# Layer norm statistics by accumulating passes of ScalarE beside a causal attention, and a projection that leaves PSUM by ScalarE

## The chip, the cores and the metric

The kernel runs on 1 core of one Trainium2 chip. The metric is the device time of one launch in microseconds (us). Before the change it is 2574.32 us, the median of 3 runs (2571.3 to 2575.26).

## The reference

The input x has 4096 rows of 256 numbers, all in float32. Two residual layers follow each other, and each normalises on the way in and on the way out:

```python
x = x + layernorm(attention(layernorm(x)))
x = x + layernorm(ffn(layernorm(x)))
# attention: 16 heads of 16 features, causal, softmax(q k^T / 4) v, with bias b_attn,
#            then the projection  out @ w_proj + b_proj
# ffn: silu(x w1) * (x w2), two hidden layers 1024 x 1024 with gelu, then w3 (ternary weights, scales)
# layernorm(x) = (x - mean) / sqrt(variance + 1e-5), over the 256 features
```

The change concerns two of the four layer norms: the one before the attention and the one after the projection.

## The kernel before, in words

The rows are cut into 8 query blocks of 512 rows (QB), each of 4 tiles of 128 rows (NT). The attention goes over items (j, g): query block j from 0 to 7, and within it the head groups g from 0 to 3, with 4 heads each. An item has 4(j+1) steps kt, one for each tile of 128 keys. Each step issues, in this order, on the in-order queues of the engines:

- a first unit of maxima of an item to come (`MaxUnit`, L496): two products q k on TensorE (PE) into banks pm (L508), and two row maxima by VectorE (DVE, L521; on the diagonal L525 with the mask). Per step there are two such units, so four maxima. The banks come from `ps_m`, a ring of 3.
- two score units (`ScoreUnit`, L568): products s on PE (L591), less the maximum by a second product, and the exponential on ScalarE (ACT, L606). They use the ring `ps_s` of 2 double banks. On the diagonal GpSimd (POOL) zeroes what lies beyond it (L611).
- the second unit of maxima, and then the product with v of the step before (`Values.step`, L632, matmuls av L641). When an item is done, ACT copies av to SBUF (L650) and SP sends it to DRAM (`weighed`).
- some pieces of background work, and every fourth step one piece of `halve_weights` (L665) on POOL, which rounds weights for the feed-forward.

The order is written out by hand (manual schedule); nothing is reordered afterwards. `Background` (L27) holds a list of generators with a size each. `pace` (L57) draws, at the end of each step, as many pieces as the sum of the sizes divided by the steps that are left, rounded up; these steps are those of the items up to g = 2 of the block. So the sizes in

```python
PREP, PROJECT, NORM = 22, 20, 12
```

(L183) set how many pieces a step draws, and with that when each piece is issued. Two generators run beside each query block:

- `project(j, room)` (L185) projects the block that has just been finished. It reads the sums of the softmax back from DRAM (L191), takes their reciprocal on DVE (L194), sends that to DRAM and reads it back spread out (L201), multiplies on POOL (L208), multiplies by w_proj in two halves of two tiles on PE (L218), adds the bias and takes the statistics on DVE (L226, L138, L139), and normalises and adds x on POOL (L149, L238). The PSUM bank of a half comes from `ps_s`, shared with the scores.
- `prep(j)` (L433) prepares the block two further on: layer norm statistics on DVE (L138, L139), normalising on POOL, transposes, and the products that give k, q and v (`features`, L361), whose evacuation is done by ACT (L375, L478).

Where a generator yields `BESIDE`, one unit of maxima that is due later is issued between (`unit_beside`, L741): beside query blocks 1 to 6, up to four pairs a block. The first two `prep` run before the attention begins. The last projection runs beside the feed-forward, which comes after the attention (`feed_forward`, L848).

The statistics before the change are two DVE operations for a tile, and 1/sqrt is one DVE and one POOL operation:

```python
nc.vector.bn_stats(st, src)
nc.vector.bn_aggr(mv[:, t, :], st)
...
nc.vector.tensor_scalar_add(ve, mv[:, :, 1], EPS)
nc.gpsimd.tensor_tensor(rstd, ve, neghalf, ALU.pow)
```

Of the kernel before, what the change touches and what calls it, by code (L numbers as in the profile page):

```python
# [10 lines left out]
F32 = mybir.dt.float32  # L11
F32R = mybir.dt.float32r
AF = mybir.ActivationFunctionType
ALU = mybir.AluOpType
# [3 lines left out]
P = 128  # L18
QB = 512
NT = QB // P  # L20
NEG = -1.0e30
EPS = 1e-5
# [45 lines left out]
def sandwich_kernel(  # L68
# [19 lines left out]
    nc = tc.nc  # L88
    S, D = x.shape
# [6 lines left out]
    NB = S // QB  # L96
# [4 lines left out]
    const = ctx.enter_context(tc.tile_pool(name="const", bufs=1))  # L101
# [4 lines left out]
    stat = ctx.enter_context(tc.tile_pool(name="stat", bufs=3))  # L106

    def rows(src, j):
        return src[j * QB : (j + 1) * QB, :].rearrange("(t p) d -> p t d", p=P)

    def load_block(j, src=x):
        t = xpool.tile([P, NT, D], F32, tag="x", name=f"x{j}")
        nc.sync.dma_start(out=t, in_=rows(src, j))
        return t
# [18 lines left out]
    neghalf = const.tile([P, NT], F32, tag="neghalf", name="neghalf")  # L133
    nc.gpsimd.memset(neghalf, -0.5)

    def layernorm_stats(src, mv, t):
        st = stat.tile([P, nc.vector.BN_STATS_DIM], F32, tag="bn", name="bn")
        nc.vector.bn_stats(st, src)  # L138
        nc.vector.bn_aggr(mv[:, t, :], st)  # L139

    def layernorm_rstd(mv):
        ve = stat.tile([P, NT], F32, tag="ve", name="ve")
        nc.vector.tensor_scalar_add(ve, mv[:, :, 1], EPS)  # L143
        rstd = stat.tile([P, NT], F32, tag="rstd", name="rstd")
        nc.gpsimd.tensor_tensor(rstd, ve, neghalf, ALU.pow)  # L145
        return rstd

    def normalize(dst, src, mv, rstd, t, engine=nc.vector):
        engine.tensor_scalar(  # L149
            dst, src, mv[:, t, 0:1], rstd[:, t : t + 1], ALU.subtract, ALU.mult  # L150
        )
# [27 lines left out]
    bp = const.tile([P, D], F32, tag="bp", name="bp")  # L179

    weighed = [scratch.tile([G, P, QB], F32, tag=f"av_{j}", name=f"avd_{j}") for j in range(NB)]
    inverse = [scratch.tile([H, QB], F32, tag=f"inv_{j}", name=f"invd_{j}") for j in range(NB)]
    PREP, PROJECT, NORM = 22, 20, 12  # L183

    def project(j, room):  # L185

        xj = load_block(j)

        sums = stat.tile([P, H * QB // P], F32, tag="sums", name=f"sums_{j}")
        heads = weighed[j].rearrange("g (h e) n -> (g h) e n", e=HW)  # L190
        nc.sync.dma_start(out=sums, in_=heads[:, HD, :].rearrange("h (a n) -> h a n", a=8))  # L191
        for _ in range(3):
            yield True
        nc.vector.reciprocal(sums, sums)  # L194
        yield True
        nc.sync.dma_start(out=inverse[j].rearrange("h (a n) -> (h a) n", a=8), in_=sums)
        oT, inv = room.features(j)
        for c in range(DC):
            mine = slice(8 * c, 8 * (c + 1))
            nc.sync.dma_start(out=oT[:, c, :], in_=heads[mine, 0:HD, :])  # L200
            nc.sync.dma_start(  # L201
                out=inv[:, c, :],
                in_=inverse[j][mine, None, :].to_broadcast([8, HD, QB]),
            )
        for _ in range(4):
            yield True
        for c in range(DC):
            nc.gpsimd.tensor_tensor(oT[:, c, :], oT[:, c, :], inv[:, c, :], ALU.mult)  # L208
            yield True
        for _ in range(2):  # L210
            yield True
        y = room.tokens(j)
        mv = stat.tile([P, NT, 2], F32, tag="mv", name=f"mvy_{j}")
        for half in range(0, NT, 2):
            ps = room.bank(f"py_{j}_{half}").rearrange("p (t f) -> p t f", t=2)
            for t in range(2):
                for c in range(DC):
                    nc.tensor.matmul(  # L218
                        ps[:, t, :],
                        lhsT=oT[:, c, (half + t) * P : (half + t + 1) * P],  # L220
                        rhs=wp[:, c, :],
                        start=(c == 0),
                        stop=(c == DC - 1),
                    )
                yield Background.BESIDE
            nc.vector.tensor_tensor(  # L226
                y[:, half : half + 2, :],
                ps,
                bp[:, None, :].to_broadcast([P, 2, D]),
                ALU.add,  # L230
            )
            for t in range(2):
                layernorm_stats(y[:, half + t, :], mv, half + t)
            yield True
        rstd = layernorm_rstd(mv)
        for t in range(NT):
            normalize(y[:, t, :], y[:, t, :], mv, rstd, t, nc.gpsimd)
            nc.gpsimd.tensor_tensor(y[:, t, :], y[:, t, :], xj[:, t, :], ALU.add)  # L238
            yield True
        nc.sync.dma_start(out=rows(x1[j], 0), in_=y)  # L240
        yield True
# [36 lines left out]
    with ExitStack() as actx:  # L278
# [13 lines left out]
        def two_banks(name):  # L292
            return ps_s.tile([P, 2, QB], F32, tag="s", name=name)

        class Room:
# [5 lines left out]
            def features(self, j):  # L301
                return [wk1.tile([P, DC, QB], F32, tag=t, name=f"{t}_{j}") for t in ("o", "inv")]
# [130 lines left out]
        def prep(j, engine=nc.gpsimd):  # L433

            xj = xb[j] if j in xb else load_block(j)
            for _ in range(3):
                yield True
            mv = stat.tile([P, NT, 2], F32, tag="mv", name=f"mv_{j}")
            for t in range(NT):
                layernorm_stats(xj[:, t, :], mv, t)  # L440
                yield True
            v_j = kv.tile([P, NT, H * VW + HD], F32, tag=f"v{j}", name=f"v{j}")
            vb.append(v_j)
            nc.gpsimd.memset(v_j[:, :, H * VW :], 0.0)
            v_heads = v_j[:, :, 0 : H * VW].rearrange("p t (h e) -> p t h e", e=VW)
            nc.gpsimd.memset(v_heads[:, :, :, HD:VW], 1.0)
            rstd = layernorm_rstd(mv)
            for t in range(NT):
                normalize(xj[:, t, :], xj[:, t, :], mv, rstd, t, engine)
                yield True  # L450
            for _ in range(3):
                yield True
            xT = xTs[j] = wk1.tile([P, DC, QB], F32, tag="T", name=f"xT_{j}")
            ps = two_banks(f"pt_{j}")
            for c in range(DC):
                for t in range(NT):
                    nc.tensor.transpose(
                        ps[:, c, t * P : (t + 1) * P], xj[:, t, c * P : (c + 1) * P], ident
                    )
            nc.scalar.copy(xT, ps)  # L460
            yield True
            for s in "kq":
                for c in range(DC):
                    yield from features(j, s, c, engine)
                    yield True
            for half in range(0, NT, 2):
                ps = two_banks(f"pv_{j}_{half}")[:, 0, :].rearrange("p (t f) -> p t f", t=2)
                for t in range(2):
                    for c in range(DC):
                        nc.tensor.matmul(  # L470
                            ps[:, t, :],
                            lhsT=xT[:, c, (half + t) * P : (half + t + 1) * P],
                            rhs=wv[:, c, :],
                            start=(c == 0),
                            stop=(c == DC - 1),
                        )
                    yield Background.BESIDE
                nc.scalar.copy(  # L478
                    v_heads[:, half : half + 2, :, 0:HD],
                    ps.rearrange("p t (h d) -> p t h d", d=HD),  # L480
                )
                yield True
# [256 lines left out]
        ahead, begun_pair, item = [], [], (0, 0)  # L739
# [14 lines left out]
        ps = two_banks("pb")[:, 0, 0:D]  # L754
# [93 lines left out]
    def feed_forward(halves):  # L848
# [6 lines left out]
        with ExitStack() as fctx:  # L855
# [189 lines left out]
```

## Time and profile before

| | |
|---|---|
| median of 3 runs | 2574.32 us |
| the profiled execution | 2574.63 us, its span 2572.9 us |
| mean granted TensorE clock | 0.966 |
| matmuls of PE, busy | 2439.2 us (95%) |
| DVE, busy | 1824.1 us (71%) |
| ACT, busy | 1257.2 us (49%) |
| POOL, busy | 575.2 us (22%) |
| L521, maxima of 128x512 on DVE | 1792 times, 1112.4 us busy |
| L606, exponentials on ACT | 1175 times, 1040.6 us busy |
| L138, statistics of x in `prep`, `norm_block` | 64 times, 415 ns each |
| L138, statistics of y in `project` (7 blocks) | 28 times, 411 ns each |
| L139, their aggregation | 181 to 184 ns each |
| L226, bias of the projection on DVE | 14 times, 682 ns each |

A line of the profile gives the engine, the source line, the operation, what it writes and reads (`y<-py,bp`: y from py and bp), its shape and how often it occurs. In a timeline the first two numbers are the start and the duration in us, and the bracket at the end is the time for which the engine had been idle, with what ended that wait. PEld is the loading of weights into PE, SPq the queue from which DMAs are issued. The length of a step can be read from the starts of successive groups of eight av matmuls (L641): there are 4608 of them, eight for each of the 576 steps. The attention spans the first 1851 us; the feed-forward follows.

### The profile page before, as it was taken

The page shows a single profiled execution, that of the slowest core. Times are in us where ns is not written, and L with a number is a line of the kernel's source. Part 1 is how long each engine was busy: PE and PEld are TensorE (multiplying, and loading weights), DVE is VectorE, ACT ScalarE, POOL GpSimd, SP SyncE. Part 2 cuts the span into 40 slices and gives each one's busy share as a digit, 9 for nine tenths or more (in the row PEclk, how much of TensorE's full clock was granted, in tenths as well). Part 3 has the DMA queues.
Part 4 walks back from the last instruction along what each step waited for, and adds up shares of the span by engine and source line. Part 5 has one row for each costly group of instructions (what it writes and reads, how often), then busy time and mean ns, then how long its engine had stood idle before and what let it go on. Part 6 is the DMA issues. An engine that isn't in the chain of part 4 may idle for free. (4 is left out here: it accounts for less than half of the span.)

```text
span 2572.9 us, 40118 instructions
## 1 busy us (share of the span) xinstructions
PE 2439.2 (95%) x15237; PEld 1444.8 (56%) x15237; DVE 1824.1 (71%) x3965; ACT 1257.2 (49%) x1490; POOL 575.2 (22%) x869
## 2 busy tenths in 40 slices
PE   5899999999999999999999999999989999999998
PEld 2454445445445544554455554544468877887786
DVE  2687788879788987898899898986055445544553
ACT  1335466556566655666577666766712222222221
POOL 2325333332242234322322222000120000000000
PEclk8779899899999999999999999999999999999999
DMA  4444244232233323324212232111120000000000
GB/s 156 144 152 154 88 135 153 99 129 74 91 108 123 120 83 130 109 79 141 66 62 95 83 96 72 57 45 55 42 90 17 17 1 17 17 17 1 17 9 10
DMA packets 134777, 202.73 MB, mean 79 GB/s; under 512 B 14864, under 2 KB 59536, under 8 KB 134576
## 3 DMA queue, kind: packets, MB, share of 16 engines
q1 hardware_dynamic: 132624, 198.75, 23.3%
q8 instruction: 122, 2.00, 0.3%
q10 hardware_dynamic: 1776, 1.18, 0.2%
q0 software_dynamic: 176, 0.15, 0.1%
q14 instruction: 79, 0.65, 0.1%
HBM read 137.91 MB, written 62.13 MB: 78 GB/s over the span
## 5 line engine op out<-in xcount | busy, mean ns | idle before, releaser
L606 ACT ACTIVATE e<-s 128x1024 f32<-128x1024 f32 (+3 forms) x1175 | 1040.6, 936 | 618.5 <-PE s L591 611.5
L521 DVE TENSOR_REDUCE mx<-pm 128x1 f32<-128x512 f32 x1792 | 1112.4, 682 | 160.4 <-PE pm L508 145.8
L508 PE MATMUL pm<-k,q 64*128 64x512 f32 (+3 forms) x2304 | 636.8, 460 | 56.8 <-DVE mx L521 40.7
L508 PEld LDWEIGHTS pm<-k,q 64*128 64x128 f32 x2304 | 326.5, 190 | 567.3 <-DVE mx L521 394.7
L641 PE MATMUL av<-e,v 128*32 128x512 f32 (+3 forms) x4608 | 591.1, 584 | 2.9 <-POOL e L611 2.9
L591 PE MATMUL s<-q,k 64*128 64x512 f32 (+3 forms) x2304 | 476.3, 395 | 7.6 <-DVE y L226 3.1
L591 PE MATMUL s<-mrow,ones 64*128 64x512 f32 (+3 forms) x2304 | 461.6, 384 | 0.0
L525 DVE CUSTOM_DVE_ANT_0 pm<-pm,mask 128x384 f32<-128x384 f32 (+3 forms) x512 | 239.8, 517 | 75.3 <-PE pm L508 71.4
L974 ACT ACTIVATE fb<-z,sh 128x512 f32<-128x512 f32 x128 | 88.1, 688 | 396.6 <-PE z L940 377.8
L591 PEld LDWEIGHTS s<-q,k 64*128 64x128 f32 x2304 | 237.0, 191 | 79.0 <-issue 19.3
L591 PEld LDWEIGHTS s<-mrow,ones 64*128 64x128 f32 x2304 | 241.8, 191 | 38.6 <-DVE mrow L565 0.7
L611 POOL TENSOR_SCALAR_AFFINE_SELECT e<-e 128x256 f32<-128x256 f32 x256 | 102.2, 407 | 647.6 <-ACT e L606 645.9
L145 POOL TENSOR_TENSOR rstd<-ve,neghalf 128x4 f32<-128x4 f32 x32 | 32.9, 1027 | 847.7 <-DVE ve L143 822.1
L940 PE MATMUL z<-hb_0h,h 128*128 128x512 f32 x512 | 203.7, 398 | 0.0
L940 PE MATMUL z<-hb_0l,h 128*128 128x512 f32 x512 | 202.2, 395 | 0.0
L641 PEld LDWEIGHTS av<-e,v 128*32 128x32 f32 x4608 | 92.6, 109 | 148.8 <-issue 130.0
L910 DVE CAST hb_1h<-fb 128x512 fp32r<-128x512 f32 x64 | 27.4, 428 | 149.9 <-ACT fb L974 149.9
L910 DVE CAST hb_0h<-fb 128x512 fp32r<-128x512 f32 x64 | 27.5, 430 | 139.4 <-ACT fb L974 139.4
L940 PEld LDWEIGHTS z<-hb_0h,h 128*128 128x128 f32 x512 | 96.8, 189 | 22.9
L940 PEld LDWEIGHTS z<-hb_0l,h 128*128 128x128 f32 x512 | 96.8, 189 | 22.1
L959 ACT ACTIVATE sl<-za,s 128x512 f32<-128x512 f32 x64 | 44.1, 689 | 131.4 <-DVE fa L961 66.4
L693 POOL CAST wh<-wc 128x256 fp32r<-128x256 f32 x88 | 34.9, 397 | 261.8 <-DMA wc<-in_h_t_dram 197.1
(235 smaller groups left out, 2430.9 us busy)
## 6 DMA issues: line engine op xcount, KB each, us to landing
k<-k SPq DMA_DIRECT2D x288, 256.0 KB
q<-q SPq DMA_DIRECT2D x64, 256.0 KB
x<-in_x_dram SPq DMA_DIRECT2D x16, 512.0 KB
k<-hik SPq DMA_DIRECT2D x32, 256.0 KB
k<-lok SPq DMA_DIRECT2D x32, 256.0 KB
q<-hiq SPq DMA_DIRECT2D x32, 256.0 KB
q<-loq SPq DMA_DIRECT2D x32, 256.0 KB
avd<-av_sb SPq DMA_DIRECT2D x32, 256.0 KB
```

What stands on the lines that cost most here:

```text
L508: nc.tensor.matmul(ps[:, 0:n], lhsT=qT[j, g][pr][r, t * P : (t + 1) * P], rhs=kT[G * j + g, c, pr][r, 0:n], start=True, stop=True,)
L521: nc.vector.tensor_reduce(self.mx[:, h, c : c + 1], ps[:, 0:n], AX.X, ALU.max)
L525: nc.vector.tensor_tensor_reduce(out=ps[:, 0:n], in0=ps[:, 0:n], in1=mask[:, QB - n : QB], scale=1.0, scalar=-3.0e38, op0=ALU.add, op1=ALU ...
L591: nc.tensor.matmul(self.ps[i][:, self.q0 :], lhsT=(self.k, ones[pr])[m][r, :], rhs=(qT[j, g][pr], mT[j, g])[m][r, self.q0 :], start=(m == ...
L606: nc.scalar.activation(e[:, at : at + n, q0:], ps[:, :, q0:], AF.Exp)
L611: nc.gpsimd.affine_select(out=at, in_=at, compare_op=ALU.is_ge, fill=0.0, base=0, pattern=[[0, 2], [1, P]], channel_multiplier=-1,)
L641: nc.tensor.matmul(self.av[h * HW : (h + 1) * HW, q0:], lhsT=vb[kt // NT][:, kt % NT, o : o + HW], rhs=es[h // 2][:, h % 2, q0:], start=(k ...
L693: nc.gpsimd.tensor_copy(hi, w)
L910: nc.vector.tensor_copy(hi, full)
L940: nc.tensor.matmul(ps, lhsT=w[c], rhs=single(part[:, c, :]), start=(c == 0 and i == 0), stop=(c == kc - 1 and i == parts - 1),)
L959: nc.scalar.activation(sl, za, AF.Silu, scale=s1[:, oc : oc + 1])
L974: nc.scalar.activation(h, z, AF.Gelu, scale=sc[:, oc : oc + 1])
```

## The change

In `prep` for blocks 2 to 7 and in `project` for blocks 0 to 6, that is wherever they run beside the attention, the statistics are taken by two passes of ACT over each tile. The first gives minus the mean as the accumulated sum of -x/256. The second squares x plus that value, and accumulates the sum of squares. Between the two passes, and after each, the generator yields. The small operation ahead of 1/sqrt goes to POOL and does the division by 256; the normalising on POOL adds instead of subtracting. In `project` a half of the product leaves PSUM by a copy on ACT, and the bias is added on POOL, in place, in SBUF. The statistics of all four tiles come after both halves. The sizes of the two generators grow by the added yields. The first two `prep`, the last `project` and `norm_block` keep the operations of before.

```diff
+    def mean_of(src, mv, t):
+
+        junk = const.tile([P, D], F32, tag="junk", name="junk")
+        nc.scalar.activation(
+            junk, src, AF.Identity, scale=-1.0 / D, accum_out=mv[:, t, 0:1]
+        )
+
+    def spread_of(src, mv, t):
+
+        junk = const.tile([P, D], F32, tag="junk", name="junk")
+        nc.scalar.activation(
+            junk, src, AF.Square, bias=mv[:, t, 0:1], accum_out=mv[:, t, 1:2]
+        )
+
+    def rstd_of(mv):
+
+        ve = stat.tile([P, NT], F32, tag="ve", name="ve")
+        nc.gpsimd.tensor_scalar(ve, mv[:, :, 1], 1.0 / D, EPS, ALU.mult, ALU.add)
+        rstd = stat.tile([P, NT], F32, tag="rstd", name="rstd")
+        nc.gpsimd.tensor_tensor(rstd, ve, neghalf, ALU.pow)
+        return rstd
+
+    def shift_and_scale(dst, src, mv, rstd, t, engine):
+        engine.tensor_scalar(
+            dst, src, mv[:, t, 0:1], rstd[:, t : t + 1], ALU.add, ALU.mult
+        )
...
-    PREP, PROJECT, NORM = 22, 20, 12
+    PREP, PROJECT, NORM = 26, 28, 12
...
+        last = j == NB - 1
...
-            nc.vector.tensor_tensor(
-                y[:, half : half + 2, :],
-                ps,
-                bp[:, None, :].to_broadcast([P, 2, D]),
-                ALU.add,
+            if last:
...
+            else:
+                nc.scalar.copy(y[:, half : half + 2, :], ps)
+                nc.gpsimd.tensor_tensor(
+                    y[:, half : half + 2, :],
+                    y[:, half : half + 2, :],
+                    bp[:, None, :].to_broadcast([P, 2, D]),
+                    ALU.add,
+                )
+            yield True
+        if not last:
+            for t in range(NT):
+                mean_of(y[:, t, :], mv, t)
+                yield True
+                spread_of(y[:, t, :], mv, t)
+                yield True
+        rstd = (layernorm_rstd if last else rstd_of)(mv)
+        for t in range(NT):
+            (normalize if last else shift_and_scale)(
+                y[:, t, :], y[:, t, :], mv, rstd, t, nc.gpsimd
             )
-            for t in range(2):
-                layernorm_stats(y[:, half + t, :], mv, half + t)
-            yield True
-        rstd = layernorm_rstd(mv)
-        for t in range(NT):
-            normalize(y[:, t, :], y[:, t, :], mv, rstd, t, nc.gpsimd)
...
+            ahead = j < 2
             for t in range(NT):
-                layernorm_stats(xj[:, t, :], mv, t)
+                if ahead:
+                    layernorm_stats(xj[:, t, :], mv, t)
+                else:
+                    mean_of(xj[:, t, :], mv, t)
+                    yield True
+                    spread_of(xj[:, t, :], mv, t)
                 yield True
...
-            rstd = layernorm_rstd(mv)
+            rstd = (layernorm_rstd if ahead else rstd_of)(mv)
             for t in range(NT):
-                normalize(xj[:, t, :], xj[:, t, :], mv, rstd, t, engine)
+                (normalize if ahead else shift_and_scale)(
+                    xj[:, t, :], xj[:, t, :], mv, rstd, t, engine
+                )
                 yield True
```

More of the change, by code (lines that the diff above doesn't have):

```diff
@@ L225, in project @@
                 yield Background.BESIDE
-            nc.vector.tensor_tensor(
-                y[:, half : half + 2, :],
-                ps,
-                bp[:, None, :].to_broadcast([P, 2, D]),
-                ALU.add,
-            )
-            for t in range(2):
-                layernorm_stats(y[:, half + t, :], mv, half + t)
-            yield True
-        rstd = layernorm_rstd(mv)
-        for t in range(NT):
-            normalize(y[:, t, :], y[:, t, :], mv, rstd, t, nc.gpsimd)
+            if last:
+                nc.vector.tensor_tensor(
+                    y[:, half : half + 2, :],
+                    ps,
+                    bp[:, None, :].to_broadcast([P, 2, D]),
+                    ALU.add,
+                )
+                for t in range(half, half + 2):
+                    layernorm_stats(y[:, t, :], mv, t)
+            else:
+                nc.scalar.copy(y[:, half : half + 2, :], ps)
+                nc.gpsimd.tensor_tensor(
+                    y[:, half : half + 2, :],
+                    y[:, half : half + 2, :],
+                    bp[:, None, :].to_broadcast([P, 2, D]),
+                    ALU.add,
+                )
[10 more added lines that the diff above has]
+                y[:, t, :], y[:, t, :], mv, rstd, t, nc.gpsimd
+            )
             nc.gpsimd.tensor_tensor(y[:, t, :], y[:, t, :], xj[:, t, :], ALU.add)
@@ L446, in prep @@
             nc.gpsimd.memset(v_heads[:, :, :, HD:VW], 1.0)
-            rstd = layernorm_rstd(mv)
+            rstd = (layernorm_rstd if ahead else rstd_of)(mv)
             for t in range(NT):
-                normalize(xj[:, t, :], xj[:, t, :], mv, rstd, t, engine)
+                (normalize if ahead else shift_and_scale)(
+                    xj[:, t, :], xj[:, t, :], mv, rstd, t, engine
+                )
                 yield True
```

## The prediction

> **What bounds the kernel now.** I read the page's shares first, then the periods of the inner step over the whole attention, then the timeline of an ordinary step and of a step with a projection in it. The attention runs from about 40 to 1851 us of the span; the feed-forward after it holds no line that the change touches outside its last-block branch, so it stays as it is.
>
> ```profile
> PE 2439.2 (95%) x15237; PEld 1444.8 (56%) x15237; DVE 1824.1 (71%) x3965; ACT 1257.2 (49%) x1490; POOL 575.2 (22%) x869
> 908.00:927.00 19.00, 19.00 (x146) 9.70 (x142) 17.25 (x35) 14.01 (x15) 6.18 (x8) 1.00 0.48 145
> 927.00:948.00 21.00, 17.90 (x90) 8.49 (x92) 16.21 (x38) 6.56 (x8) 2.90 (x3) 0.92 0.00 1
> ```
>
> The second and third lines are windows: busy PE, PEld, DVE, ACT and POOL, then the granted clock. In seven ordinary steps PE is full, VectorE (DVE) has 9% left and ScalarE (ACT) 26%. In the next 21 us, with one projection, PE, DVE and ACT are all idle part of the time: they wait for each other. Ordinary step, timeline:
>
> ```profile
> 923.21 2.48 DVE L521 TENSOR_REDUCE mx<-pm 128x1 f32<-128x512 f32 x4 [0.21 <-PE pm L508]
> 923.74 1.94 ACT L606 ACTIVATE e<-s 128x1024 f32<-128x1024 f32 x2 [0.76 <-PE s L591]
> 924.38 0.16 PEld L641 LDWEIGHTS av<-e,v 128*32 128x32 f32 x8 [0.25 <-issue]
> 925.38 0.18 PEld L508 LDWEIGHTS pm<-k,q 64*128 64x128 f32 x2 [0.84 <-DVE mx L521]
> 925.91 2.48 DVE L521 TENSOR_REDUCE mx<-pm 128x1 f32<-128x512 f32 x4 [0.22 <-PE pm L508]
> ```
>
> The period is 925.91 - 923.21 = 2.70 us: four maxima at 0.62 (2.48) and 0.22 of waiting for the next products, while ACT does two exponentials (1.94) and waits 0.76. PE and DVE bound each other through the three PSUM banks of pm. The step with half a projection:
>
> ```profile
> 927.09 1.06 PE L641 MATMUL av<-e,v 128*32 128x512 f32 x8
> 931.16 1.29 DVE L521 TENSOR_REDUCE mx<-pm 128x1 f32<-128x512 f32 x2 [0.20 <-PE pm L508]
> 932.36 0.68 DVE L226 TENSOR_TENSOR y<-py,bp 128x512 f32<-128x512 f32 x1
> 932.90 2.14 ACT L606 ACTIVATE e<-s 128x1024 f32<-128x1024 f32 x2 [4.52 <-PE s L591]
> 933.08 0.43 DVE L138 BATCH_NORM_STATS2 bn<-y 128x6 f32<-128x256 f32 x1
> 934.07 0.18 DVE L139 BATCH_NORM_AGGREGATE mvy<-bn 128x2 f32<-128x6 f32 x1
> 934.17 0.54 DVE L525 CUSTOM_DVE_ANT_0 pm<-pm,mask 128x384 f32<-128x384 f32 x1
> 934.82 0.18 PEld L508 LDWEIGHTS pm<-k,q 64*128 64x128 f32 x1 [1.14 <-DVE mx L525]
> 935.20 1.06 PE L641 MATMUL av<-e,v 128*32 128x512 f32 x8
> ```
>
> From 932.36 to 934.17 DVE does the bias addition and the statistics; behind them stand the maxima, whose bank PE needs at 934.82, and behind that the next av. This is the stretch that the change empties.
>
> **What the Trainium skill says.** "ScalarE: Activation LUTs", section What ACT_TABLE_LOAD costs: 186 ns and 0.833 ns per element, some 93 more for each pointer operand. The trace agrees: 382 ns for 256 elements of e (399 by the rule), 687 for 512 with a bias pointer (706). "VectorE: DVE Perf Modes", section Two Vector instructions with no wait between them: an operation that also writes its accumulator is two instructions; here 141 ns for DVE's read. For ScalarE's no run here shows it. "TensorE: Matmul & The Clock Gate", Part 1: the clock falls to half after an idle window of about 3.4 us. The trace has such pieces of 3.4 and 6.8 us, one at 943.6, just after a projection. "SBUF — State Buffer", section Who interferes with whom: DVE disturbs GpSimd (POOL) only with two SBUF inputs or in its two-port modes; the maxima read PSUM, so I charge nothing.
>
> **The change, part by part.** The profiled execution took 2574.63 us (span 2572.9), 0.3 above the median 2574.32; I sum against it. (j,g) is query block and head group, a step one kt; blocks are named by the attention that runs (beside block j, block j-1 is projected).
>
> 1. Projection halves, 14. Per half, 0.68 (L226), twice 0.43 (L138) and twice 0.18 (L139), 1.81 in all overlapped, leave DVE. The block's maxima then follow at 932.45; the bank is free 0.62 later, PE's second pm of that unit at 933.3 and av at 933.55 instead of 935.20: 1.65 less. The next half (943.44 - 935.20 = 8.24) comes to the same 6.5: 1.75 less. The features' steps, built alike but evacuated by ACT, take 6.31 and 6.43 (av at 1001.57, 1007.88, 1014.31), which speaks for it. Blocks 1 to 6: 6 x 3.4 = 20.4. Block 7 has no maxima units slipped between (steps of 6.04 and 5.98); the second pm moves from 1551.82 to 1550.75: 2 x 1.1 = 2.2. Together -22.6. The new PSUM copy is L650's kind (593 ns for 128x512) and runs at about 930.7 to 931.3, in ACT's 4.52 of waiting: nothing; without that cover 14 x 0.59 = 8. The bank is given back earlier than by L226.
> 2. Half-clock pieces after projections: the excess of steps over their like is 2.3 in block 3, 1.5 in 5, 1.6 and 1.3 in 6: 6.7. With PE idle less, I take -5 (0 to -6.7).
> 3. Preparation of blocks 2 to 7: 24 pairs of statistics leave DVE. A step with one takes 2.92 instead of 2.70: the pair's 0.44 fills the 0.22 first. Where DVE is never idle the whole 0.44 counts: 24 x 0.22 to 0.44 = 5.3 to 10.6. With 13 of L143's 0.16, I take -8.
> 4. ACT: 52 mean and 52 spread passes over 256 elements. 0.38 to 0.47 by the rows above, the spread with its bias pointer, and an accumulator read that I price as DVE's 0.14: 0.55 and 0.65. Below: 0.38 (no separate read). Above: 1.0, if the read and the wait of the spread for the mean cost 0.3 more. From block 3 on one goes into each step, behind both exponentials: 0.65 against 0.76 of waiting. It costs nothing there; e is read by av a step later (e ended 1.4 before av), and its bank is wanted 0.5 after it is free, so even 0.85 would only pile up slowly. In blocks 1 and 2 the larger sizes (28 and 26) draw two or three pieces a step: some 16 steps with two passes, 1.25 - 0.76 = 0.5 over, 8; less the 0.5 of slack in each of four rows and the longer steps of block 1: +4 (0 to 10). The built program has no further table load.
> 5. POOL: 14 additions over 128x512, 1.28 each by L208's row, and 13 small operations (0.1 to 1.0). POOL is 22% busy and had been idle 24.8 us before it worked on this projection. Behind the addition stand the casts of the weights and the next selects; ACT's first mean waits for it, but a step (2.7 us) lies between. The scaling moves past diagonal steps in blocks 4 to 6 and leaves them in block 3: 0 (-1 to +4).
> 6. Moved pieces. The order of the built program has the reciprocal (L194) one step earlier in blocks 1 and 3, the projection three steps earlier in block 1 (kt 4 instead of 7) and five in block 3. Its transfers come no earlier: in SP's queue the sums' read stands behind the landing of av. DVE waited 0.37 and 1.22 there; now a step more, 2 x 2.7. In block 1 the products for c=1 are ready at 176.1 (L208), and PE would arrive near 172.7: 3.5 of stall. In block 3 they are ready at 460.6, PE comes at 460.7: nothing. Sum +9 (0 to 12). Such waits brought half-clock pieces in blocks 2, 4 and 6 (waits of 2.6 to 4.5): +3 (0 to 6).
>
> Sum: -22.6 - 5 - 8 + 4 + 9 + 3 = -19.6; 2574.6 - 19.6 = 2555.0 us. What is late next, once DVE is free in a projection step: PE itself (two times 1.06 of py, 0.43 and more of pm, 0.93 of s, 1.0 of av), so no more than this can come.
>
> **The rivals.**
> - More: all waits of step 6 but PE's stall are hidden, the half-clock pieces go, ACT costs nothing: -22.6 - 6.7 - 10 + 6 = -33, 2541. For it: 9% of DVE idle even in ordinary steps. Against: the reciprocal waited in all seven blocks.
> - Nothing: PE at 95% is the bound and what DVE gives up was overlapped; half of parts 1 and 3 remains (-15.3), no clock piece goes, the waits come (+12): 2571. Against: PE falls to 85% in the projection's window.
> - Slower: ACT becomes the bound. If a pass with its accumulator and its wait takes 1.25 us, each of the 104 is 0.49 over the 0.76 of the step: +51 in the steps of preparation and projection, in place of the +4. -35.6 + 12 + 51 = +27, 2602. It decides from about 0.98 a pass, where 104 x 0.22 eats the 23.6 that the rest leaves. For it: no accumulating pass in this trace, and ACT is in order with e behind it. Against: the rows of ACT leave 0.5 us for what I cannot see.
> - That the change doesn't do what it says is excluded by the built order: 104 passes and 14 copies on ACT, 131 rows fewer on DVE.
>
> **How the numbers follow.** About 0.2% (5 us) is what a measurement of this kernel can tell from no change. Forecast (2544 to 2568) 0.62; more (2535 to 2544) 0.12; nothing (2568 to 2580) 0.13; slower (above 2580) 0.13. Faster: 0.62 + 0.12 + 0.02 of the third = 0.76; same 0.11; slower 0.13. The range cuts the second in half (0.06) and leaves out the fourth and the edge of the third (0.14): 2540 to 2576.
>
> **What would show it.** Right: projection steps near 6.5 (block 7: 5), preparation steps back at 2.70, ACT's passes at 0.5 to 0.7 with no exponential waiting for one, longer waits of L194 in blocks 1 and 3 only, fewer half-clock pieces. Wrong: passes near 1 us, exponentials waiting for POOL's addition, projection steps still at 8.

## The result and the profile after

The changed kernel takes 2537.03 us, the median of 5 runs (2530.97 to 2540.4), against 2575.26 of the kernel before in the same series (5 runs). The ratio is 0.985, with a 95% interval of 0.9835 to 0.9864: 35 to 42 us faster. The forecast was 2555.0, with a range of 2540 to 2576. So the sign was right, and the gain, 19.6 in the forecast, is twice as large. The profiled execution took 2537.64 us (span 2535.9). The shares of its page:

```profile
PE 2415.0 (95%) x15237; PEld 1437.1 (57%) x15237; DVE 1787.8 (70%) x3834; ACT 1310.2 (52%) x1712; POOL 561.0 (22%) x896
```

DVE lost 36 us of work and ACT gained 53. POOL, which got 14 additions, has 14 us less; why is in the last section. The windows that answer to the two of before, seven ordinary steps of block 5 and then 21 us with both halves of a projection (busy PE, PEld, DVE, ACT, POOL, then the granted clock):

```profile
887.20:906.20 19.00, 19.00 (x146) 9.66 (x142) 17.03 (x34) 14.08 (x15) 5.28 (x6) 1.00 0.44 129
906.20:927.20 21.00, 20.14 (x130) 10.54 (x129) 17.37 (x35) 12.32 (x19) 7.91 (x10) 1.00 0.04 14
```

The ordinary stretch is as it was. In the other, PE went from 17.90 to 20.14 busy and the clock from 0.92 to 1.00. The step with the first half, as a timeline:

```profile
906.29 1.06 PE L696 MATMUL av<-e,v 128*32 128x512 f32 x8
909.94 0.58 ACT L266 COPY y<-py 128x512 f32<-128x512 f32 x1 [2.35 <-PE py L248]
910.36 1.29 DVE L576 TENSOR_REDUCE mx<-pm 128x1 f32<-128x512 f32 x2 [0.20 <-PE pm L563]
910.60 1.27 POOL L267 TENSOR_TENSOR y<-y,bp 128x512 f32<-128x512 f32 x1 [12.87 <-ACT y L266]
911.57 0.56 DVE L580 CUSTOM_DVE_ANT_0 pm<-pm,mask 128x384 f32<-128x384 f32 x1
912.10 1.94 ACT L661 ACTIVATE e<-s 128x1024 f32<-128x1024 f32 x2 [1.58 <-PE s L646]
912.14 0.54 PE L563 MATMUL pm<-k,q 64*128 64x384 f32 x2
912.61 1.07 PE L696 MATMUL av<-e,v 128*32 128x512 f32 x8
```

From av to av it is 912.61 - 906.29 = 6.32 us, where it was 8.11; the forecast had 6.46. Between the maxima of 910.36 and those of 911.57 nothing stands on DVE, ACT copies the bank in a wait that it had anyway, and PE's products of 912.14 follow each other without a wait. In block 7 the two steps are 4.62 and 4.63 (6.04 and 5.98 before; forecast about 4.9). Ordinary steps on ACT, with a pass in each:

```profile
925.58 0.42 ACT L144 ACTIVATE junk<-y 128x256 f32<-128x256 f32 x1
925.89 0.20 ACT L144 ACTIVATION_READ_ACCUMULATOR junk<-y 128x1 f32 x1
926.47 1.94 ACT L661 ACTIVATE e<-s 128x1024 f32<-128x1024 f32 x2 [0.37 <-PE s L646]
928.29 0.51 ACT L151 ACTIVATE junk<-y,mvy 128x256 f32<-128x256 f32 x1
928.69 0.20 ACT L151 ACTIVATION_READ_ACCUMULATOR junk<-y,mvy 128x1 f32 x1
929.17 1.94 ACT L661 ACTIVATE e<-s 128x1024 f32<-128x1024 f32 x2 [0.28 <-PE s L646]
```

The exponentials start at 926.47 and 929.17, 2.70 apart, and still wait for PE, not PE for them.

For the whole attention I use one measure in what follows. The length of each of its 575 steps is read from the starts of av. For each step I take the shortest length that this same step has in any trace of this study, and call what a trace has above it its excess. A piece at half clock is a stretch of time in which the granted TensorE clock is 0.5. The table has the means of three traces of each kernel (the two further ones are the last experiment), by what the step holds, each step counted once; in brackets the us that PE ran at half clock in these steps. The fourth row holds all of PE's background products but the projection's.

| steps with | before | after | difference | forecast |
|---|---|---|---|---|
| a half of the projection, and the two steps behind | 86.3 (41.0) | 49.7 (3.4) | -36.6 | -22.6 - 5 + 3.5 (block 1's stall) = -24.1 |
| the reciprocal, and the two behind | 19.4 (14.8) | 27.5 (22.8) | +8.1 | +5.4 + 3 = +8.4 |
| statistics or passes | 9.6 (2.1) | 6.2 (5.9) | -3.4 | -8 + 4 = -4 |
| the preparation's products | 64.0 (7.5) | 66.1 (9.4) | +2.1 | 0 |
| none of these | 18.5 (42.5) | 10.4 (29.9) | -8.1 | 0 |
| sum | 197.8 (107.9) | 159.9 (71.4) | -37.9 | -19.7 |

The feed-forward, from the start of the last step's av to the end of the span, did not change: 721 to 725 us in all six.

### The profile page after: what moved, and what is told of

Read it like the earlier page. It is cut to its first block, busy times and chain, and to the rows that moved or that the text cites. A ratio compares the mean times of both kernels' runs of the same rounds, so it can differ in the third digit from the quotient of the medians.

```text
span 2535.9 us, 40119 instructions
## 1 busy us (share of the span) xinstructions
PE 2415.0 (95%) x15237; PEld 1437.1 (57%) x15237; DVE 1787.8 (70%) x3834; ACT 1310.2 (52%) x1712; POOL 561.0 (22%) x896
## 5 line engine op out<-in xcount | busy, mean ns | idle before, releaser
L563 PE MATMUL pm<-k,q 64*128 64x512 f32 (+3 forms) x2304 | 627.2, 455 | 44.8 <-DVE mx L576 33.0
L696 PE MATMUL av<-e,v 128*32 128x512 f32 (+3 forms) x4608 | 584.4, 579 | 1.5 <-POOL e L666 1.5
L172 POOL TENSOR_TENSOR rstd<-ve,neghalf 128x4 f32<-128x4 f32 x19 | 19.3, 1015 | 687.3 <-DVE ve L170 661.6
L995 PEld LDWEIGHTS z<-hb_0l,h 128*128 128x128 f32 x512 | 97.1, 190 | 22.6
L995 PEld LDWEIGHTS z<-hb_0h,h 128*128 128x128 f32 x512 | 97.1, 190 | 22.6
```

The source lines that it names most:

```text
L563: nc.tensor.matmul(ps[:, 0:n], lhsT=qT[j, g][pr][r, t * P : (t + 1) * P], rhs=kT[G * j + g, c, pr][r, 0:n], start=True, stop=True,)
L696: nc.tensor.matmul(self.av[h * HW : (h + 1) * HW, q0:], lhsT=vb[kt // NT][:, kt % NT, o : o + HW], rhs=es[h // 2][:, h % 2, q0:], start=(k ...
L995: nc.tensor.matmul(ps, lhsT=w[c], rhs=single(part[:, c, :]), start=(c == 0 and i == 0), stop=(c == kc - 1 and i == parts - 1),)
```

## The experiments

Each ran on the chip in 4 to 22 runs beside the kernel before, in the same series; the last four only once each. Ratios are to the kernel before; a difference to the changed kernel is that of the ratios times 2574. First the theory at this point: the parts of the sum that concern DVE are right, and the half clock gave more than was written down. Rival: the waits of the moved pieces (+12 in the sum) never came, or came cheaper.

**The places alone** (`v_places`):

```diff
-            if last:
+            if True:
...
-            for t in range(NT):
-                mean_of(y[:, t, :], mv, t)
+            for _ in range(2 * NT):
                 yield True
-                spread_of(y[:, t, :], mv, t)
-                yield True
...
-                if ahead:
-                    layernorm_stats(xj[:, t, :], mv, t)
-                else:
-                    mean_of(xj[:, t, :], mv, t)
+                layernorm_stats(xj[:, t, :], mv, t)
+                if not ahead:
                     yield True
-                    spread_of(xj[:, t, :], mv, t)
...
```

> The order of pieces of the changed kernel, with the engines of the kernel before: bias and statistics on VectorE where they stood, empty pieces in place of ScalarE's passes, the larger sizes. So only the moving of pieces is left. The prediction on record: longer waits for the reciprocal (+5.4), PE's stall in block 1 (+3.5) and half-clock pieces from them (+3) against a run of the kernel before: +12, about 2587. Rival: the moved waits lie beside other work or replace old ones, within 4 us of the kernel before: 2571 to 2579; then these terms of the sum were wrong.

Measured: 2599.41 us, ratio 1.010 (1.0081 to 1.0119), 26 slower than before. Both expectations were too low, and the rival is out: the moved pieces cost. By the measure above (against the mean of before) +6 lies with the projections, +7 with the reciprocals and +11 with the statistics, which the larger sizes put elsewhere; half clock rose to 151 us. The changed kernel pays as much at the reciprocals (+8) and has 3 less at the statistics, which ACT takes there. So this run bounds the cost of the places; it doesn't give the share of it in the changed kernel.

**One part at a time** (`v_project`, `v_prep`). For the first, `prep` is put back as it was, with its size 22; for the second, `project`, with its size 20:

```diff
-    PREP, PROJECT, NORM = 26, 28, 12
+    PREP, PROJECT, NORM = 22, 28, 12
...
-    PREP, PROJECT, NORM = 26, 28, 12
+    PREP, PROJECT, NORM = 26, 20, 12
...
```

> Only the projection's part: PSUM copy and statistics on ScalarE, bias on GpSimd; preparation stays on VectorE as before (size 22). Prediction on record: -22.6 -5 for the halves and the clock, +12 for moved pieces, +2 for ScalarE: about 2561. Rival (moved pieces and passes cost next to nothing, the clock gives back up to 10): -33, about 2542.

Measured: 2546.19 us, ratio 0.990 (0.9882 to 0.9917): -26.

> Only the preparation's part: 24 pairs of statistics on ScalarE (size 26), the projection as before. Prediction on record: -8 for VectorE, +2 for ScalarE in blocks 1 and 2, with some moved pieces: about 2569. Rival: the passes cost nothing and the clock pieces in steps with two diagonal maxima go too: about 2562 to 2565. If the two parts add up to the whole, project and prep alone together give 38 less than the kernel before; if they share a gain, more.

Measured: 2563.9 us, ratio 0.9969 (0.9956 to 0.9981): -8. The forecast's -6 for the preparation is in the interval (-5 to -11). The projection's part is worth some 12 more than the -13.6 of the sum. Both together are -34, with an uncertainty of about 5; the whole change is -39. They share no gain that can be seen, and most of what the forecast lacked lies with the projection.

**The bias left on DVE** (`v_bias_dve`): PSUM copy and addition as before, statistics on ACT.

```diff
-            if last:
+            if True:
                 nc.vector.tensor_tensor(
...
-                for t in range(half, half + 2):
-                    layernorm_stats(y[:, t, :], mv, t)
+                if last:
+                    for t in range(half, half + 2):
+                        layernorm_stats(y[:, t, :], mv, t)
```

> The changed kernel with the PSUM bank of the projection left by VectorE with the bias, as before; only the statistics of the projection on ScalarE. If the halves' steps are set by everything that VectorE does between the units of maxima (the prediction's chain), 14 x 0.68 = 9.5 come back: 2546. Rival: only the statistics stood in the way, since the maxima's banks wait for PE at that place anyway: 2537 to 2540. The steps of the halves show it: 7.1 against 6.45.

Measured: ratio 0.9873 (0.9853 to 0.9892), 2540.09 us: +6 on the changed kernel, between the two; the intervals overlap, so the time alone decides nothing. The steps do: the first half's step in block 5 is 6.94 long instead of 6.32. DVE in it:

```profile
915.27 1.29 DVE L577 TENSOR_REDUCE mx<-pm 128x1 f32<-128x512 f32 x2 [0.20 <-PE pm L564]
916.48 0.68 DVE L257 TENSOR_TENSOR y<-py,bp 128x512 f32<-128x512 f32 x1
917.07 0.56 DVE L581 CUSTOM_DVE_ANT_0 pm<-pm,mask 128x384 f32<-128x384 f32 x1
```

The addition sits between the maxima, as in the kernel before, and blocks 4 to 6 have 1.2 more each, 0.6 a half, near its 0.68; block 7 has 0.2 a half. In the kernel before, with the half clock gone (the run after next), the projection's steps of blocks 5 and 6 hold 11.1 of excess, with the change 7.5: 3.6 a block for a forecast of 3.4, of which 1.2 is the bias and 2.4, the rest, the statistics.

**The statistics of the projection on DVE, in later steps** (`v_stats_dve`):

```diff
             for t in range(NT):
-                mean_of(y[:, t, :], mv, t)
+                layernorm_stats(y[:, t, :], mv, t)
                 yield True
-                spread_of(y[:, t, :], mv, t)
                 yield True
...
```

> The changed kernel, but the statistics of the projection's rows are taken by VectorE, in pieces of their own behind the halves (28 pairs in ordinary steps, where the two ScalarE passes stood); PSUM copy and bias stay as changed. If VectorE has 0.22 us free in a step, each pair costs 0.22 to 0.44: +6 to +12 on the changed kernel, 2543 to 2549. Rival: it was enough that they left the projection's own steps: 2535 to 2540.

Measured: 2560.35 us, ratio 0.9949 (0.9936 to 0.9962): +25 on the changed kernel, more than both said. The steps with statistics or passes have 23.9 of excess in place of 6.2: 17.7 for 28 pairs, 0.63 a pair instead of 0.22 to 0.44, with 10 us more of half clock among them; another 5 lie with the projection's steps. So it matters that they left DVE and not only that they left the projection's steps.

**TensorE's wait filled** (`v_fill`), in the kernel before:

```diff
                 layernorm_stats(y[:, half + t, :], mv, half + t)
+            fill.append(2)
             yield True
...
-                    issue(MaxUnit(*pairs[0][1]))
+                    issue(MaxUnit(*pairs[0][1]), fill.pop() if fill else 0)
...
                 for i, ps in enumerate(self.ps.values()):
                     r = slice(i * P // 2, (i + 1) * P // 2)
-                    nc.tensor.matmul(
+                    for _ in range(1 if i else 1 + again):
+                        nc.tensor.matmul(
...
```

> The kernel before, but TensorE's wait for VectorE in the step behind each half of the projection is filled: the first product of that step's second unit of maxima is issued three times with the same result (two times 0.43 us of work for nothing, in the 0.76 to 1.2 of waiting). VectorE's work is left as it was. Theory (the half-clock pieces behind the projections come from TensorE's idling there, and cost about 0.43 us of time for each us): the 44 us of half clock beside and behind the projections go, and with them 10 to 15 us: 2556 to 2564 against 2574 of before. Rival (the clock has nothing to do with that idling, and the gain of the change is VectorE's emptied chain alone): 2572 to 2580.

Measured: ratio 0.9985 (0.9975 to 0.9995), 2569.13 us: -4, less than the theory's -10 to -15 and yet not nothing. The trace says where. First the two halves of block 6 and the step behind in the kernel before (busy PE, PEld, DVE, ACT, POOL, granted clock), then the same with the wait filled:

```profile
1222.10:1230.30 8.20, 6.71 (x33) 3.23 (x32) 6.62 (x14) 3.34 (x4) 0.00 (x0) 1.00 0.00 1
1230.30:1240.20 9.90, 8.42 (x35) 3.80 (x34) 6.67 (x14) 2.05 (x2) 0.00 (x0) 0.83 0.00 0
1240.20:1244.20 4.00, 4.00 (x21) 1.97 (x20) 2.51 (x8) 0.85 (x1) 2.35 (x3) 0.57 0.12 30
```

```profile
1220.60:1228.80 8.20, 7.19 (x35) 3.61 (x34) 6.62 (x14) 3.37 (x4) 0.00 (x0) 1.00 0.01 2
1228.80:1237.10 8.30, 7.27 (x39) 3.65 (x40) 6.72 (x15) 2.05 (x2) 0.00 (x0) 1.00 0.01 2
1237.10:1239.60 2.50, 2.50 (x24) 1.34 (x23) 2.41 (x8) 0.53 (x1) 1.04 (x1) 1.00 0.00 0
```

DVE's work is the same 6.6 to 6.7 in each half, and PE has 0.5 more of useless work in the first. The granted clock stays at 1.00, and the three stretches take 19.0 us instead of 22.1. In blocks 4 to 6 the 13.6 us of half clock around the projections (17.0 and 13.6 in the two further traces of the kernel before) are gone, and the second half and the step behind are 5.5 shorter over the three blocks (38.8 to 33.3 by av starts), 0.40 for each us of half clock. In blocks 1 to 3 most of the half clock stayed (31 us before, 22 here). In blocks 1 and 2 both halves fall into one step; that PE idles there at other waits too, which this filling doesn't reach, is only an argument. In the same trace the reciprocal's steps, which the filling does not touch, have 5 us more than in the kernel before, with 6 more at half clock; why is open, and in this trace it takes back what blocks 4 to 6 gained. So shown, by one trace against three: idling of PE beside DVE's chain brings half-clock pieces in blocks 4 to 6, and they cost time of their own beside the wait. For blocks 1 to 3 it isn't shown by this run.

**The subtracting form on GpSimd** (`v_subtract`): the mean kept positive.

```diff
-            junk, src, AF.Identity, scale=-1.0 / D, accum_out=mv[:, t, 0:1]
+            junk, src, AF.Identity, scale=1.0 / D, accum_out=mv[:, t, 0:1]
...
-            junk, src, AF.Square, bias=mv[:, t, 0:1], accum_out=mv[:, t, 1:2]
+            junk, src, AF.Square, scale=-1.0, bias=mv[:, t, 0:1], accum_out=mv[:, t, 1:2]
...
-            dst, src, mv[:, t, 0:1], rstd[:, t : t + 1], ALU.add, ALU.mult
+            dst, src, mv[:, t, 0:1], rstd[:, t : t + 1], ALU.subtract, ALU.mult
```

> The changed kernel with the mean kept positive, so that GpSimd normalises by subtract and multiply as before (1.22 us for 128x256 in both traces of that form) instead of add and multiply (0.55): 52 x 0.67 = 35 us more of GpSimd. If the shorter GpSimd operation is where the gain beyond the forecast came from (it stands ahead of the diagonal selects and of the transposes), 8 to 18 us come back: 2545 to 2555. Rival: GpSimd is 22% busy and nothing waits for it: 2536 to 2539, half-clock pieces apart.

Measured: ratio 0.9867 (0.9852 to 0.9881), 2539.79 us. The interval overlaps that of the changed kernel, so nothing or a few us (the ratios differ by 4). POOL's longer work is hidden, and it isn't where the gain came from.

**Twice the passes** (`v_double`): each of the two `activation` calls stands twice.

```diff
+        nc.scalar.activation(
+            junk, src, AF.Identity, scale=-1.0 / D, accum_out=mv[:, t, 0:1]
+        )
...
+        nc.scalar.activation(
+            junk, src, AF.Square, bias=mv[:, t, 0:1], accum_out=mv[:, t, 1:2]
+        )
```

> The changed kernel with each of the 104 accumulating passes issued twice, so 1.2 to 1.4 us of ScalarE in a step in place of 0.6 to 0.7. The prediction's slower rival counts what lies over the 0.76 of waiting in a step, 0.49 each, as time: +51, 2588. Rival: the steps that draw a pass follow steps with none or lie in longer steps, and the exponentials' 5 buffers take the delay: under +15, below 2552.

Measured: 2559.69 us, ratio 0.9946 (0.9932 to 0.9959): +25 on the changed kernel, half of the rule's +51 and above the rival's 15. ACT in two ordinary steps:

```profile
935.59 0.42 ACT L144 ACTIVATE junk<-y 128x256 f32<-128x256 f32 x1
935.90 0.20 ACT L144 ACTIVATION_READ_ACCUMULATOR junk<-y 128x1 f32 x1
936.13 0.42 ACT L147 ACTIVATE junk<-y 128x256 f32<-128x256 f32 x1
936.46 0.19 ACT L147 ACTIVATION_READ_ACCUMULATOR junk<-y 128x1 f32 x1
936.55 1.92 ACT L667 ACTIVATE e<-s 128x1024 f32<-128x1024 f32 x2
938.36 0.51 ACT L154 ACTIVATE junk<-y,mvy 128x256 f32<-128x256 f32 x1
...
939.50 1.92 ACT L667 ACTIVATE e<-s 128x1024 f32<-128x1024 f32 x2
```

Two passes hold ACT for 936.55 - 935.59 = 0.96 (mean) and 939.50 - 938.36 = 1.14 (spread), 1.05 on the mean, since neighbours overlap; and two exponentials hold it for 1.81, not 1.94. ACT never waits here, and yet steps with passes in blocks 3 to 7, those at full clock, are 2.72 to 2.83 long on each block's mean with doubled passes, against 2.69 to 2.78 with single ones. The +51 took 1.25 for two passes; with the measured 1.05 and 1.81, 0.16 over a step of 2.70, the same rule gives 104 x 0.16 = 17, less than was lost. The cost lies elsewhere than the rule has it: 8 in block 1 and 6 in block 2, where several passes fall into one step, and 3 in block 0; blocks 3 to 7 together have 2, where the rule gives 64 x 0.16 = 10. So the rule of the rival, what lies over the wait counts as time, fails for rows of 8 to 16 steps with one doubled pass each, and undercounts where pieces are crowded. That the five buffers of the exponentials carry the delay through such a row is argued; their number was not varied.

**The reciprocal later** (`v_late`, `v_before_late`): three pieces more ahead of it, with the size grown by three, in the changed kernel and in the kernel before.

```diff
-        for _ in range(3):
+        for _ in range(6):
             yield True
         nc.vector.reciprocal(sums, sums)
```

> The changed kernel with the reciprocal three pieces later (6 empty pieces ahead of it, size 31), so that the sums have landed when VectorE comes to it. If VectorE's waiting there (23.9 us in 7 blocks) is on the path, the steps with a reciprocal (4 to 7 us) come back towards 2.7: -12 to -20, 2517 to 2525. Rival: the wait lies beside other work, or the projection is late elsewhere then (the items up to the third head group must hold all pieces): within 5 us of 2537.

Measured: 2509.41 us, ratio 0.975 (0.9738 to 0.9763): 26 less than the changed kernel, more than expected. Changed kernel first, DVE's wait for the landing of the sums over the whole run (us, times, longest), then this one, from the tile's own view (us, times):

```profile
DVE sums L224 <- DMA sums<-avd: 23.9, 7, 7.0
```

```profile
  DMA sums<-avd: 1.5, 2
```

The reciprocal's group of steps falls from 27.5 of excess (22.8 us at half clock) to 1.4 (none). The wait was on the path, with its half clock. But the 26 us of the run are not these 26: at the new place the projections' steps hold 61 instead of 50, with 17 us at half clock instead of 3, the steps with passes 6 more, and the attention as a whole is 12 shorter, at the low end of the -12 to -20. The other half lies in the feed-forward, which takes 710 us instead of 721 to 725, and which the expectation did not have. The longest wait above, 7.0, is that of the last reciprocal, which stands in DVE's queue beside the feed-forward. It is 0.9 now; PE is busy for 94.9 of the first 100 us after the attention instead of 87.6, and the half-clock pieces between 28 and 83 us behind the last av are gone.

> The kernel before with the reciprocal three pieces later, nothing else. In the trace of before, the steps with a reciprocal and the two behind each hold 20.6 us over their fastest like, half clock included. If this wait was on the path in the kernel before as well: -15 to -25, 2549 to 2559, with no other part of the change. Rival: later projections of blocks 1 to 3 cost as much by other waits: within 6 us of 2574.

Measured: 2561.1 us, ratio 0.9954 (0.9941 to 0.9967): -12, less than expected. The reciprocal's group falls from 19.4 to 1.1 here too, but the projections of the kernel before rise from 86 to 94 at the new place and the statistics from 10 to 14, so that the attention is only 3 shorter. The rest is the feed-forward again (713 us, the last reciprocal waiting 3.0 instead of 7.6 to 8.1). So inside the attention the same shift pays 12 once DVE's chain is gone and 3 before; beside the feed-forward it pays 11 to 12 in both kernels.

**Further shifts** (`v_late2`, `v_late3`): on top of the later reciprocal, three pieces more ahead of POOL's multiplication, in all blocks, or in blocks 2 and 3 alone.

```diff
-        for _ in range(4):
+        for _ in range(7):
...
+        for _ in range(7 if j in (1, 2) else 4):
```

> The changed kernel with the reciprocal three pieces later, and three pieces more between it and GpSimd's multiplication (size 34). In the trace with the later reciprocal alone (2509 us), TensorE still stands 3 to 4 us in blocks 1 to 3 for the multiplication, which waits for the landing of the spread inverse, with half-clock pieces there. If these stalls go: -8 to -14 on that, 2495 to 2502. Rival: the pieces behind the projection are pressed into fewer steps in blocks 1 and 2, two or three accumulating passes a step, and ScalarE is late: 2505 to 2515.

Measured: 2515.13 us, ratio 0.977 (0.9757 to 0.9783), its rival's side. The projections' group falls from 61 to 48, and the steps with passes and those with none of the listed things rise by 12, so the attention is as long as with the later reciprocal alone (+1). The feed-forward, whose projection is delayed as well, is 7 longer (717 us), and that is the difference between the two runs.

> The changed kernel with the reciprocal three pieces later everywhere, and the further three pieces ahead of GpSimd's multiplication only in blocks 2 and 3, where the run with both shifts had blocks 4.3 us shorter each than the run with the later reciprocal alone (block 1 was 4.3 longer there). If the blocks stand for themselves: 8 less than the later reciprocal alone, 2498 to 2504. Rival: what that run lost elsewhere (half-clock pieces in untouched steps of block 6, 10 us of them) belongs to the shift and not to chance: 2508 to 2515.

Measured: 2506.38 us, ratio 0.9736 (0.9719 to 0.9752), between the two expectations. The feed-forward is at 711 us again, the attention 3 shorter than with the later reciprocal alone. The whole can't be told from that run's time; these two are the fastest of the study, 26 and 29 us under the changed kernel.

**Both kernels traced again** (`again_before_1`, `again_after_1`, `again_before_2`, `again_after_2`), unchanged.

> The kernel before, traced again. If half-clock pieces in block 0 and the last item of block 6 belong to the program: 38 and 10 us of them as in the first trace. If chance: other numbers there, while the projections' steps hold 35 to 55 us again (44 in the first trace). Time 2565 to 2579.

> The changed kernel, traced again. If the pieces belong to the program: 25 us in block 0 and none in the last item of block 6, as in the first trace. If chance: other numbers there, while the projections' steps hold at most 15 us again (10 in the first trace). Time 2531 to 2541.

> The kernel before, traced a third time, with the same expectation as the second: 38 and 10 us of half clock in block 0 and the last item of block 6 if they belong to the program, other numbers if they are chance; 35 to 55 us in the projections' steps.

> The changed kernel, traced a third time, with the same expectation as the second: 25 us of half clock in block 0 and none in the last item of block 6 if they belong to the program, other numbers if they are chance; at most 15 us in the projections' steps.

Measured: 2569.1 and 2572.7 us before, 2530.07 and 2532.26 after. Half clock, first trace and the two new ones:

| us at half clock | before | after |
|---|---|---|
| the projections' steps | 44.4, 41.0, 37.5 | 10.2, 0, 0 |
| block 0, steps of none of these kinds | 38.4, 34.0, 33.3 | 25.2, 27.3, 24.6 |
| block 6, steps of none of these kinds | 10.2, 3.4, 3.4 | 0, 6.8, 0 |

Block 6's pieces are chance. Those of block 0 belong to the program. The projections' are the largest item, and there the two kernels are apart in each trace.

## Why the prediction was too small, step by step

1. The halves: right. 3.6 a block against 3.4, and 2.7 in block 7 against 2.2: 24.3 in place of 22.6. The 3.6 is measured in blocks 4 to 6 and taken over for blocks 1 to 3, of which no trace of the kernel before is free of half clock.
2. The half clock after projections, "-5 (0 to -6.7)": this step failed. The mechanism was right, its size was not. I listed the excess of steps in blocks 3, 5 and 6 only, and part of it. The trace of before had it in six blocks. By the lengths of the second halves and the steps behind, over their like, it is 1.1 in block 1, 2.6 in 2, 5.3 in 3, 1.4 in 4, 1.5 in 5 and 3.2 in 6: 15, of which I had 6.7 as the most. The same count over the three traces of before, with the steps of the filled run as the like in blocks 4 to 6, gives 13; the 37.6 us of half clock that the first row loses, at 0.40, give 15. With 13 to 15 in place of 5 that row closes: -24.3 - 13 (or 15) + 2 for block 1's stall is -35 to -37, and -36.6 was measured. That PE's idling brings such pieces, and that they go with it, was shown in blocks 4 to 6 by the filled wait; in blocks 1 to 3 it is argued from the changed kernel, in which they go too, but for 10.2 us in block 1 in one of three traces. "TensorE: Matmul & The Clock Gate", Part 1, speaks of a free-running window and of idle ones, and its section "A second HAM failure mode: psum-queue depth-cycling" of short idling, often enough. Here, in block 5, the clock fell behind two steps in which PE was 81% busy (13.20 of 16.30 us) and never waited over 0.8 us at a time. That agrees with the second. The prediction quoted the idle window alone, and of single long waits there are none in these two steps.
3. The preparation's statistics, -8, and 4, ACT's passes, +4: together -3.4 for -4. An accumulating pass is 0.42 or 0.51 and its read 0.20; with the overlap a pass holds ACT for about 0.48 or 0.57, under the 0.55 and 0.65 that I priced. "ScalarE: Activation LUTs", What ACT_TABLE_LOAD costs, has a rule from which 399 ns for 256 elements and 492 with a pointer operand can be estimated; the trace has 418 and 510. In blocks 3 to 7 the passes cost next to nothing.
5. POOL, 0: right, within the few us that the subtracting form leaves open. Its busy time fell by 14 us instead of rising; the sum did not have the shorter operation of the last section.
6. The moved pieces, +9 and +3: right in sum, and nearly so term by term. The reciprocal's steps got 8.1 longer for 8.4 in the forecast. On the mean of the three traces DVE's waits for the sums in blocks 1 to 7 grew from 12.56 to 17.43 us, 4.9 for the 5.4, and half clock by 8.0, at 0.40 worth 3.2 for the 3. They did so mostly where it was said: +5.1 in block 3, +2.5 in block 1, +0.5 in all others. One reading was wrong: the reciprocal did not wait "in all seven blocks" but in six of them, and the seventh of its waits, 7.6 us, is the one beside the feed-forward, which the change leaves as it is. PE's stall in block 1, forecast at 3.5, is 2.4 in the first trace of after and 1.3 in the two others; in the first, waits of PE from 155 to 200 us (us, times, longest):

```profile
PE py L248 <- POOL o L238: 2.4, 2, 2.0
```

What is left, -6 of the table's last two rows, has no term in the sum: 3 lie in block 0 with its half clock, which is less in every trace of the changed kernel, and also in the run whose preparation stayed on DVE. What makes it less is open. The rest is spread over several blocks, and its cause is open too.

The rivals: "more" (2541) had the clock among its reasons, but took 6.7 for it and reached its number with waits that were to vanish, and they did not. That 2537 lies near it is luck. "Nothing" and "slower" are out. The point of the last one, 0.98 a pass, from which nothing of the gain was to be left, was not tested as such; at 1.05 a step 25 us are lost of 39, and the kernel is still 14 faster than before.

## What to carry to other kernels

Half-clock pieces are priced from a list of all of them, each with the steps it touches, before anything is put down as a small correction: here they were 8 to 10 of the 18 us that the forecast lacked. An emptied wait on the engine that feeds TensorE is worth the wait and the clock that goes with it, and another wait on the same path can become worth more: inside the attention the later reciprocal paid 3 us before the change and 12 after it, so a shift that paid little is tried again. A saving is then looked for in every stage, also where nobody expected it: half of that run's 26 us lay beside the feed-forward. An overload of an in-order engine by 0.16 us a step cost little here through rows of 8 to 16 steps; crowded pieces did cost.

## What the runs showed of the hardware

GpSimd normalises 128x256 by add and multiply in less than half the time that it needs for subtract and multiply. Groups of the kernel before, the changed kernel, and the changed kernel with the subtracting form (busy, mean ns):

```profile
L149 POOL TENSOR_SCALAR y<-y,mvy,rstd 128x256 f32<-128x256 f32 x28 | 34.3, 1224 | 0.8
```

```profile
L164 POOL TENSOR_SCALAR y<-y,mvy,rstd 128x256 f32<-128x256 f32 x28 | 15.6, 556 | 0.8
```

```profile
L164 POOL TENSOR_SCALAR y<-y,mvy,rstd 128x256 f32<-128x256 f32 x28 | 34.3, 1226 | 0.8
```

Same operands and shapes, and the form alone moves it from 556 to 1226 ns. On ACT the accumulator of a pass is read by an instruction of its own, 0.20 us, as on DVE (0.14).
